# Two transformer blocks on one core: the end of unit 6's routing is moved into the wait for unit 7's projection

## The chip, the cores and the metric

One NeuronCore of a Trainium2 chip runs the whole program. TensorE (PE) multiplies matrices and transposes; VectorE (DVE), ScalarE (ACT) and GpSimd (POOL) work on tiles; SyncE (SP) and GpSimd issue DMAs. The metric is the device time of one execution in microseconds (us). All arithmetic is in 32-bit floats.

## The reference, cut to what matters

The input is 8 rows of 512 tokens with 256 channels. Four layers are added to it in turn, each on a layer norm of what is there:

```
x = x + attention0(norm(x))      # relative positions, 16 heads, softmax over 512 keys
x = x + ffn0(norm(x))            # 256 -> 1024 -> 256, weights changed per row
x = x + attention1(norm(x))      # attends over the 8 rows, at each token position
x = x + moe(norm(x))             # 32 experts, 4 chosen per token, and a shared expert
```

The change lies at the end of attention1 and in the routing of moe. For each token, routing computes 32 scores, keeps two of four groups of experts, takes the best four experts, and scales their outputs by their scores' shares:

```
logits = tokens @ router_weight.T ; scores = sigmoid(logits)
topk_idx = top 4 of (scores + bias), in the two best of four groups
topk_w = scores[topk_idx] / sum * 2.5
mixed = sum over the 4 of expert(token) * topk_w
```

## The kernel before, in words

**Units.** The last two layers are worked in 8 units of 512 tokens (u = 0..7): two rows of the input and half of each row's token positions, as four tiles of 128 tokens. `attend` (L1403) plans the attention of a unit and `routed` (L1427) its routing, which runs beside the attention of the next unit. After unit 7's attention comes its routing with no other unit beside it, then the experts.

**An order written out by hand.** Each step is given a planned time by `at` (L1375). The events are sorted by that time and emitted one after the other; the times only set the order in which each engine's instructions stand. `hop` (L1378) plans a step that is written as a generator: its first part at `first`, the rest at `then`. So TensorE's part can stand early and VectorE's later. In the built program, an instruction that nothing holds can stand earlier on its engine than its event: before the change, the four idle matmuls planned just before unit 7's transposes stand among the last transposes of its attention.

**Attention of unit 7.** `weighted` (L1081) multiplies values by their softmax weights on VectorE, eight times (m = 0..7); the tile `value` has three buffers. `gathered` (L1092) adds their transposes up on TensorE (`ao`), and after the last one ACT copies the sum (`aoT`, L1110). `projected` (L1122), for r = 0 and 1, multiplies by the projection matrix on TensorE (`po`, L1127) and adds the result to x on VectorE.

**Routing.** `measure2` (L1140) takes mean and variance of the four tiles on VectorE (L53, L54, L56) and the root of the variance on GpSimd (`rstd`, L58, a power of -0.5). `norm2` makes `shift` on VectorE and the normed tiles `xn` on ACT (L1149). `turn2` transposes them (`pt`, L1161; `xT`, L1162); `logits` and `scores` follow (L1169, L1173). `route` chooses the experts on VectorE; `count` and `take` place them among all tokens. `send` (L1269) has a first part on TensorE (`pk`, L1276 to L1278) and a second on VectorE: `rule`, `bounds`, `key`, `tops`, `slot` (the rows to which the tokens go), then `eq`, `weight`, and into the tile `pay` the weights and the tokens' numbers (`pay<-weight`, `pay<-dest`). `copied` (L1153) copies `xn` four times into `pay` on ACT, once for each of the four chosen experts. `pay` has one buffer.

**Scatters.** At its end `send` appends 16 scatters to a list. Each is an indirect DMA issued by GpSimd (L941) that writes 128 rows of `pay` to the rows named by `slot`, into a table in DRAM sorted by expert. `pace` (L955) takes two of them off the list and emits them, and makes them wait for the last VectorE instruction emitted so far. In the last unit this extra wait is left out (`free`).

**Fillers.** `busy(n)` (L962) emits n matmuls whose result nobody reads (`idle`, L966). With `behind`, the first waits for the instructions given.

**The seam to the experts.** Unit 6's shared expert is kept for the end (`late_shared`). When unit 7's attention is over, the memory of attention is given back, and SP loads all experts' weights into it (`store`, L1487, eight DMAs). After the routing of unit 7 come the experts' page numbers, unit 6's shared expert, and fillers behind the last scatters (L1503). SP fetches the first sorted rows (`r`, L1514) after all 16 scatters of unit 7 have landed; then 160 steps, one for each page of 128 sorted rows, multiply by their expert's weights.

In line numbers of helpers: all recorded VectorE work of this stage has the line L858.

Of the kernel before, what the change touches and what calls it, by code (L numbers as in the profile page):

```python
# [863 lines left out]
def _l1(nc, tc, a, x, out, ident, mhalf, rows, results, filled, inputs, early):  # L864
# [12 lines left out]
    U = B  # L877
    seen = lambda u: 4 if u % 4 < 2 else 8
    with ExitStack() as ctx:
# [9 lines left out]
        vec = _Recorded(nc.vector)  # L889
# [43 lines left out]
        def after(ins, others):  # L933
            info = mybir.DependencyInfo(mybir.DependencyClass.Sync, mybir.DependencyReason.DATA)
            for o in others:
                tc.add_manual_dep(ins.ins, o.ins.name, info, reason="rows of DRAM")
# [25 lines left out]
        def busy(n, behind=()):  # L962

            idle = quick("idle")
            for _ in range(n):
                ins = nc.tensor.matmul(idle, inputs.wqkv[:, 0, :P], inputs.wqkv[:, 1, :S], start=True, stop=True)  # L966
                if behind:
                    after(ins, behind)
                    behind = ()

        def quick(name):

            return ps_a.tile([P, S], F32, tag="psa", name=name)

        def slow(name):

            return ps_d.tile([P, S], F32, tag="psd", name=name)
# [135 lines left out]
        def two_tiles(u, r):  # L1113
            h, p = divmod(u, 4)
            return x[2 * p + r][:, 2 * h : 2 * h + 2, :]
# [6 lines left out]
        def projected(u, r):  # L1122
            po = slow("po")
            for j in range(2):
                t = 2 * r + j
                for c in range(NK):
                    nc.tensor.matmul(  # L1127
                        po[:, j * H : (j + 1) * H],
                        turned[u][:, c, t * P : (t + 1) * P],
                        inputs.wproj[:, c, :],  # L1130
                        start=c == 0,
                        stop=c == NK - 1,
                    )
            two = two_tiles(u, r).rearrange("p t c -> p (t c)")
            vec.tensor_tensor(two, two, po, ALU.add)


        xn, xT, stats, hids, chosen, scores_of, mores, tabs = {}, {}, {}, {}, {}, {}, {}, {}

        def measure2(u):  # L1140
# [128 lines left out]
        def send(u):  # L1269

            (sel, w, share), tab = chosen.pop(u), tabs.pop(u)
            ps = slow("pk")
            pk = ps[:, : NT * NE].rearrange("p (t e) -> p t e", e=NE)
            by = ps[:, NT * NE : NT * NE + 4 * NE].rearrange("p (i e) -> p i e", e=NE)
            for i in range(4):
                nc.tensor.matmul(by[:, i, :], tab[:, i : i + 1].to_broadcast([NE, P]), ident[:NE, :NE], start=True, stop=True)  # L1276
            nc.tensor.matmul(pk, earlier, sel, start=True, stop=False)
            nc.tensor.matmul(pk, ones, past[:, NT * u : NT * u + NT, :], start=False, stop=True)  # L1278
            yield
            over = lambda i: rule[:, i, :].unsqueeze(1).to_broadcast([P, NT, NE])  # L1280
            rule = sb.tile([P, 4, NE], F32, tag="rule", name="rule", bufs=1)
            vec.tensor_copy(rule, by)
            vec.tensor_copy(bounds[:, u, :], rule[:, 3, :])
            key = sb.tile([P, NT, NE], F32, tag="key", name="key", bufs=1)
            vec.tensor_tensor(key, pk, over(1), ALU.is_lt)
            vec.tensor_tensor(key, key, over(2), ALU.mult)
            vec.tensor_tensor(key, key, pk, ALU.add)
            vec.scalar_tensor_tensor(key, key, 1.0, over(0), ALU.add, ALU.add)
            vec.tensor_tensor(key, key, sel, ALU.mult)
            top = sb.tile([P, NT, 8], F32, tag="tops", name="tops")  # L1290
            for t in range(NT):
                vec.max(top[:, t, :], key[:, t, :])
            slot = sb.tile([P, NT, TOPK], I32, tag="slot", name="slot")
            vec.tensor_scalar(slot, top[:, :, :TOPK], 1.0, None, ALU.subtract)
            eq = sb.tile([P, NT, TOPK, NE], F32, tag="eq", name="eq", bufs=1)
            vec.tensor_tensor(
                eq,
                key.unsqueeze(2).to_broadcast([P, NT, TOPK, NE]),
                top[:, :, :TOPK].unsqueeze(3).to_broadcast([P, NT, TOPK, NE]),
                ALU.is_equal,  # L1300
            )
            vec.tensor_tensor(eq, eq, w.unsqueeze(2).to_broadcast([P, NT, TOPK, NE]), ALU.mult)
            weight = sb.tile([P, NT, TOPK], F32, tag="weight", name="weight", bufs=1)
            vec.tensor_reduce(weight, eq, AX.X, ALU.add)
            vec.scalar_tensor_tensor(
                pay[:, :, :, H + 1], weight, ROUTE_SCALE, share.unsqueeze(2).to_broadcast([P, NT, TOPK]), ALU.mult, ALU.mult
            )
            vec.tensor_copy(pay[:, :, :, H].bitcast(I32), dest[:, NT * u : NT * u + NT, :])
            for t in range(NT):
                for i in range(TOPK):  # L1310
                    waiting.append(
                        partial(scatter, "rows", rows, slot[:, t, i : i + 1].bitcast(U32), pay[:, t, i, :], NS * P - 1)
                    )
# [61 lines left out]
        def at(time, f, *args):  # L1375
            events.append((time, len(events), partial(f, *args)))

        def hop(f, *args, first, then):  # L1378

            made = []  # L1380

            def begin():
                made.append(f(*args))
                next(made[0])

            at(first, begin)
            at(then, lambda: next(made[0], None))

        def prepare(u, t):

            for c in range(NK):
                at(t + 0.6 * c, turn1, u, c)
            for c in range(2 * NK):
                at(t + 1.6 + 1.9 * c + (17 if c >= NK and t > 0 else 0), project, u, c)
            for half in range(2):
                at(t + 9.3 + 1.9 * half + (17 if t > 0 else 0), tokens, u, half)
# [30 lines left out]
        def routed(u, t, n):  # L1427

            at(t + 0.2, measure2, u)
            at(t + 5.0, norm2, u)  # L1430
            if u + 1 == U:
                at(t + 8.19, busy, 4)
            at(t + 8.2, turn2, u)
            at(t + 10.0, logits, u)
            if u + 2 < U or u + 1 == U:
                at(t + 13.4, hidden, u, 0)

            rear = u + 1 == U
            if u + 2 == U:
                late_shared.append(u)  # L1440
            else:
                at(t + (31.0 if rear else 20.0), hidden, u, 1)
            split = route(u)
            at(t + 15.3, next, split)
            at(t + (21.1 if n == 8 else 19.0), next, split, None)
            late = 3.5 if n == 8 else 0.0
            hop(count, u, first=t + 23.4 + late / 2, then=t + 25.0 + late)
            if u + 2 != U:
                at(t + (30.9 if rear else 19.6 if n == 8 else 18.9), gated, u, 0)
            hop(take, u, first=t + 26.0 + late, then=t + 27.8 + late)  # L1450
            if u + 2 != U:
                at(t + (31.5 if rear else 29.5 + late), gated, u, 1)
            for i in range(TOPK):
                at(t + 24.6 + late + 1.1 * i, copied, u, i)
            hop(send, u, first=t + 28.0 + late, then=t + 30.5 + late * 1.8)
            for r in range(2 if u + 2 != U else 0):
                hop(add_shared, u, r, first=t + 32.6 + late + r, then=t + 36.5 + late * 2 + 0.7 * r)
            for i in range(8):
                at(t + 36.0 + late * 1.8 + 2.6 * i, pace, u + 1 == U)


        WAITS = {0: 5, 1: 2, 4: 5, 5: 1, 6: 3, 7: 3}
# [8 lines left out]
        for u in range(U):  # L1471
            t = start[u]
            if u + 2 < U:
                prepare(u + 2, t + 0.01)
            if u + 3 < U:
                normalized(u + 3, t + 7.6)
            attend(u, t)
            routed(u, t + T[u], seen(u + 1) if u + 1 < U else 4)
# [130 lines left out]
        with tc.manual_schedule():  # L1609


            tiles, which, rTs, made, hidTs = {}, {}, {}, {}, {}
# [172 lines left out]
```

## Time and profile before

| what | value |
| --- | --- |
| three runs | 2066.32, 2069.74, 2071.68 us (median 2069.74) |
| the profiled execution | 2061.48 us |
| its span, first to last instruction | 2059.7 us |
| mean granted TensorE clock | 0.978 of full speed |
| busy: PE, DVE, ACT, POOL | 1937.6, 1392.4, 1106.3, 1134.0 us |
| unit 7's attention and routing, until the first fetch of sorted rows | about 1680 to 1778 us |
| first matmul of the experts | 1783.08 us |

A row of the timeline gives the start from the beginning of the span, the duration, the engine, the line, the operation, the tiles (written <- read), and in brackets how long the engine sat idle before it and what released it. A row of the chain of waits gives start, duration, engine, the tile written and the line; the chain is followed back from the end of the window, at each step to what came last. "issue" means that the profile shows nothing that was waited for. In a table of stages the columns are the stage, its length, the busy time (and records) of PE, weight loads, DVE, ACT and POOL, the granted clock, the DMA engines' busy share, and GB/s. Matmuls of 32-bit floats appear as two records each or more, and a few per cent of records can be missing.

### The profile page before, as it was taken

How to read it: one execution, taken by the hardware profiler on the slowest of the kernel's cores; microseconds unless marked ns; L12 is line 12 of the kernel's file. 1: busy time of each engine (PE TensorE's matmuls, PEld its weight loads, DVE VectorE, ACT ScalarE, POOL GpSimd, SP SyncE). 2: the span in 40 equal slices, each digit the busy share in tenths (PEclk: the TensorE clock that was granted, in tenths of full speed). 3: DMA queues.
4: the chain of work that ended last, by engine and by line, in shares of the span. 5: the costliest groups of instructions: out<-in, count | busy, mean ns of one | idle time of the engine just before them, and what ended most of it. 6: DMA issues, size and time to landing. Idle time of an engine off the chain costs nothing. (4 is left out here: it accounts for less than half of the span.)

```text
span 2059.7 us, 49676 instructions
## 1 busy us (share of the span) xinstructions
PE 1937.6 (94%) x18040; PEld 1327.0 (64%) x18040; DVE 1392.4 (68%) x3727; ACT 1106.3 (54%) x2368; POOL 1134.0 (55%) x1334
## 2 busy tenths in 40 slices
PE   7999999999999999999989999999989877899997
PEld 4666666676666766766656666655555444588886
DVE  4677777677777777766776555247876786456666
ACT  3776777767777777776742211344444333144443
POOL 4666777867778677776744111014434443455555
PEclk9999999999999999999999999999999997999999
DMA  9999999999999999999974446801111114557888
GB/s 296 317 317 281 296 300 295 300 285 307 295 298 303 289 310 303 294 298 289 294 224 141 124 127 195 25 0 37 43 38 45 48 45 190 208 164 219 258 262 272
DMA packets 387522, 444.46 MB, mean 216 GB/s; under 512 B 43472, under 2 KB 368080, under 8 KB 386768
## 3 DMA queue, kind: packets, MB, share of 16 engines
q1 hardware_dynamic: 372496, 401.94, 64.3%
q0 software_dynamic: 13824, 38.29, 5.1%
q8 instruction: 146, 2.39, 0.5%
q10 hardware_dynamic: 960, 1.05, 0.2%
q14 instruction: 96, 0.79, 0.1%
HBM read 238.99 MB, written 202.19 MB: 214 GB/s over the span
## 5 line engine op out<-in xcount | busy, mean ns | idle before, releaser
L447 DVE CUSTOM_DVE_ANT_0 e<-sc,winc 128x512 f32<-128x512 f32 x512 | 333.3, 689 | 289.9 <-PE sc L433 174.1
L450 ACT ACTIVATE e<-e,low 128x512 f32<-128x512 f32 x512 | 365.6, 715 | 101.8 <-DVE low L447 100.3
L371 ACT COPY strip<-pa 128x512 f32<-128x512 f32 x512 | 275.2, 591 | 129.1 <-POOL winc L401 53.1
L374 POOL TENSOR_TENSOR own<-aside,strip 128x512 f32<-128x512 f32 x256 | 268.8, 1050 | 113.4 <-ACT strip L371 97.6
L464 DVE COPY et<-et_ps 128x512 f32<-128x512 f32 x512 | 328.5, 683 | 0.7 <-PE et_ps L461 0.7
L421 PE MATMUL sc<-sm,sm 32*128 32x256 f32 (+3 forms) x1792 | 310.0, 436 | 0.7 <-DVE low L447 0.4
L364 PE MATMUL pa<-pos,sm 32*128 32x256 f32 x2048 | 292.1, 401 | 0.1
L941 POOL DMA_INDIRECT rows<-pay,slot x128 | 141.1, 1103 | 220.3 <-issue 207.1
L401 POOL TENSOR_TENSOR winp<-winp,own 128x256 f32<-128x256 f32 x256 | 187.2, 731 | 106.3 <-DMA winp<-shift 83.7
L433 PE MATMUL sc<-ident,winp 128*128 128x128 f32 x1280 | 203.7, 287 | 30.0 <-DMA winp<-shift 29.5
L421 PEld LDWEIGHTS sc<-sm,sm 32*128 32x128 f32 x1792 | 164.3, 185 | 96.8 <-DVE et L464 35.2
L401 POOL TENSOR_TENSOR winc<-winc,own 128x256 f32<-128x256 f32 x256 | 187.1, 731 | 68.3 <-DMA winc<-shift 61.4
L941 POOL DMA_INDIRECT results<-y,r x160 | 156.3, 977 | 119.6 <-ACT y L1560 77.4
L433 PEld LDWEIGHTS sc<-ident,winp 128*128 128x128 f32 x1280 | 137.6, 142 | 108.1 <-issue 57.2
L461 PE MATMUL et_ps<-ident,e 64*128 64x64 f32 x4096 | 184.2, 230 | 1.1 <-DVE et L464 1.1
L364 PEld LDWEIGHTS pa<-pos,sm 32*128 32x128 f32 x2048 | 176.1, 185 | 10.8 <-ACT strip L371 3.9
L58 POOL TENSOR_TENSOR rstd<-var,mhalf 128x2 f32<-128x2 f32 (+1 forms) x56 | 51.0, 911 | 233.8 <-DVE var L56 210.1
L461 PEld LDWEIGHTS et_ps<-ident,e 64*128 64x128 f32 x4096 | 148.8, 140 | 44.1 <-issue 22.1
L473 PE MATMUL ctx_ps<-et,v 128*32 128x128 f32 x4096 | 168.2, 283 | 0.5 <-DVE et L464 0.5
L1540 PE MATMUL pge<-store,rT 128*128 x640 | 166.1, 382 | 1.8 <-DMA r<-rows 0.8
L174 PE MATMUL pq<-xnT,wqk 128*128 128x512 f32 x256 | 132.8, 643 | 0.7 <-PE pv L156 0.7
L738 ACT ACTIVATE hT<-ph,b 128x512 f32<-128x512 f32 x64 | 44.0, 687 | 165.6 <-PE ph L735 165.6
(222 smaller groups left out, 3340.0 us busy)
## 6 DMA issues: line engine op xcount, KB each, us to landing
shift<-strip SPq DMA_DIRECT2D x256, 510.0 KB, 4.3
winp<-shift SPq DMA_DIRECT2D x128, 384.0 KB, 4.9
winc<-shift SPq DMA_DIRECT2D x128, 384.0 KB, 6.3
winp<-shift SPq DMA_DIRECT2D x128, 256.0 KB, 4.3
winc<-shift SPq DMA_DIRECT2D x128, 256.0 KB, 4.4
rows<-empty SPq DMA_DIRECT2D x8, 2640.0 KB, 13.6
r<-rows SPq DMA_DIRECT2D x160, 132.0 KB, 2.7
z<-results SPq DMA_DIRECT2D x32, 512.0 KB, 5.6
```

The source lines that it names most:

```text
L364: nc.tensor.matmul(pa[:, t * W : (t + 1) * W], src[rs, i * P : (i + 1) * P], pos[rs, g, :], start=True, stop=True)
L371: nc.scalar.copy(st[:, 2 * j : 2 * j + 2, :].rearrange("p t w -> p (t w)"), pas[j])
L374: nc.gpsimd.tensor_tensor(own, aside.unsqueeze(2).to_broadcast([P, 2, 2, P]), st[:, :, W - 1 : W].rearrange("p (j t) o -> p t j o", t=2).t ...
L401: nc.gpsimd.tensor_tensor(dst, dst, own[:, t], ALU.add)
L421: nc.tensor.matmul(sc[:, c0:c1], s[side_][rs, cut : cut + P], s[2 + side_][rs, c0:c1], start=c0 == 0, stop=False, skip_group_check=True,)
L433: nc.tensor.matmul(sc[:, m * P : (m + 1) * P], wins[n + 2 * (m - i)][1][:, j, (i - m + 1) * P : (i - m + 2) * P], ident, start=False, stop ...
L447: nc.vector.tensor_tensor_reduce(e, sc, wins[n][0][:, j, :], 1.0, -LOW, ALU.add, ALU.min, low)
L450: nc.scalar.activation(e, e, AF.Exp, bias=low, scale=-1.0, accum_out=totals[b, g // 2][:, i, r : r + 1])
L461: nc.tensor.transpose(bank[:, c : c + 64], e[rs, m * P : (m + 1) * P], ident[rs, rs])
L464: nc.vector.tensor_copy(et[:, f].rearrange("p j m q -> p (j m q)"), bank)
L473: nc.tensor.matmul(ctx_ps[32 * r : 32 * r + 32, i * P : (i + 1) * P], vs[b % 2][:, m, g % 2, g // 2 * 4 + r, :], et[:, :, m, :], start=m = ...
L941: ins = nc.gpsimd.indirect_dma_start(to, bass.IndirectOffsetOnAxis(ap=index, axis=0), source, None, bounds_check=last)
```

## The change

For unit 6 alone, the second part of `send` is cut in two at a new `yield`. Its first piece, `rule` to `slot`, is planned at 46.05 after the start of unit 7, just ahead of unit 7's projections (46.1 and 46.8) and behind its last two `weighted`. Its second piece, `eq` to `pay<-dest`, is planned at 48.3, behind unit 7's `measure2` (48.2). All eight `pace` of unit 6 come after it, from 48.4 on; they stood from 42.3 on, 2.6 apart. In the last unit four fillers become five, and the first waits for the first residual add of unit 7's projection. Other units are unchanged: where `last` is not given, both pieces stand at `then`.

```diff
@@ projected
             vec.tensor_tensor(two, two, po, ALU.add)
+            added[u, r] = vec.last
@@ send
             vec.tensor_scalar(slot, top[:, :, :TOPK], 1.0, None, ALU.subtract)
+            yield
             eq = sb.tile([P, NT, TOPK, NE], F32, tag="eq", name="eq", bufs=1)
@@ hop
-        def hop(f, *args, first, then):
+        def hop(f, *args, first, then, last=None):
...
             at(then, lambda: next(made[0], None))
+            at(then if last is None else last, lambda: next(made[0], None))
@@ routed
             if u + 1 == U:
-                at(t + 8.19, busy, 4)
+                at(t + 8.19, lambda: busy(5, [added[u, 0]]))
             at(t + 8.2, turn2, u)
...
-            hop(send, u, first=t + 28.0 + late, then=t + 30.5 + late * 1.8)
+            if u + 2 == U:
+
+                hop(send, u, first=t + 28.0 + late, then=t + 46.05, last=t + 48.3)
+            else:
+                hop(send, u, first=t + 28.0 + late, then=t + 30.5 + late * 1.8)
...
             for i in range(8):
-                at(t + 36.0 + late * 1.8 + 2.6 * i, pace, u + 1 == U)
+                at(t + (48.4 + 0.01 * i if u + 2 == U else 36.0 + late * 1.8 + 2.6 * i), pace, u + 1 == U)
```

In the built program the order of instructions changes in this place and no other. VectorE: the five last `value` stand in one run, then `rule` to `slot`, the residual adds with their statistics and `var`, then `eq` to `pay<-dest`, then `shift`. GpSimd: `rstd` of unit 7 stands ahead of all 16 scatters of unit 6, where six stood ahead of it. TensorE: four fillers leave the last transposes of `ao`; five stand between `po` and the transposes of `xn`. The orders of ACT and SP are unchanged.

More of the change, by code (lines that the diff above doesn't have):

```diff
@@ L1135, in projected @@
             vec.tensor_tensor(two, two, po, ALU.add)
+            added[u, r] = vec.last
+        added = {}
         xn, xT, stats, hids, chosen, scores_of, mores, tabs = {}, {}, {}, {}, {}, {}, {}, {}
```

## The prediction

> **What bounds the kernel now.** TensorE is busy for 94% of the span on the page, but the change touches only the seam between the last two units and the experts, some 70 us, so I read the chain of waits there (1705 to 1785 us), then the timeline, the clock by stage and the DMA issues. First the chain:
>
> ```profile
> 1718.61 0.27 DVE pay L858 x2
> 1718.88 1.13 DVE value L858
> 1720.05 1.09 PE ao L1098 x8
> 1721.88 0.59 ACT aoT L1110
> 1722.52 2.07 PE po L1127 x8
> 1724.68 0.70 DVE x L858
> ...
> 1729.71 1.05 POOL rstd L58
> 1731.04 0.61 ACT xn L1149
> ...
> 1753.44 0.27 DVE pay L858 x2
> 1753.71 0.59 DVE hid L858
> 1754.35 3.78 PE pu L1321 x4
> ```
>
> VectorE writes unit 6's weights (pay) at 1718.61 and only then the last two values that the projection of unit 7 needs; root, norm, routing and unit 7's pay follow one behind the other. What comes after 1753.44 hangs on that write of pay on two sides: TensorE's last shared experts, and the 16 scatters of unit 7. The timeline of the other engines:
>
> ```profile
> 1720.76 1.24 POOL L941 DMA_INDIRECT rows<-pay,slot  x1 [19.92 <-issue]
> ...
> 1730.79 0.16 DVE L858 SCALAR_TENSOR_TENSOR shift<-mv,rstd 128x4 f32<-128x4 f32 x1 [2.22 <-POOL rstd L58]
> ...
> 1742.52 0.97 POOL L941 DMA_INDIRECT rows<-pay,slot  x1 [0.30 <-issue]
> ...
> 1748.32 1.05 ACT L1154 COPY pay<-xn 128x1024 f32<-128x1024 f32 x1 [0.24 <-DMA rows<-pay,slot]
> ...
> 1754.47 0.97 POOL L941 DMA_INDIRECT rows<-pay,slot  x1 [10.97 <-issue]
> 1757.65 0.98 POOL L941 DMA_INDIRECT rows<-pay,slot  x1 [2.21 <-issue]
> ...
> 1775.54 0.97 POOL L941 DMA_INDIRECT rows<-pay,slot  x1 [0.30 <-issue]
> ```
>
> These are unit 6's first and last scatter, then unit 7's. The fourth copy into pay waits for a DMA: it is let go 5.80 us after unit 6's last scatter was issued (1742.52 to 1748.32). pay has one buffer, so unit 7 may not write it while unit 6's rows are still being read. Now this wait ends 5 us before VectorE comes (1753.44). And the clock (columns: PE, weight loads, DVE, ACT, POOL busy; granted clock; DMA):
>
> ```profile
> 1732.00:1740.00 8.00, 7.73 (x26) 5.62 (x26) 1.25 (x15) 5.13 (x8) 5.87 (x7) 0.50 1.03 416
> 1756.00:1760.00 4.00, 4.00 (x9) 1.92 (x8) 0.69 (x1) 0.00 (x0) 1.95 (x2) 0.56 1.03 405
> 1760.00:1764.00 4.00, 2.51 (x12) 1.87 (x10) 2.11 (x4) 0.00 (x0) 2.92 (x3) 1.00 1.03 407
> ```
>
> After TensorE's 5.40 us pause before the first transpose (1731.70) it runs at 0.50.
>
> **The change, part by part.** The built order shows one place: on VectorE rule..slot move behind the last two values, eq..dest move behind var; on GpSimd the root moves ahead of all 16 scatters of unit 6; on TensorE four idle matmuls leave the last transposes and five come between the projection and the transposes, waiting for the first residual add.
>
> *rule..slot.* They take 1713.83 to 1716.44, 2.61 us. The values' buffers are free in time: they need the transposes of values 3 and 4, done by 1714.4. The last value ends at 1712.69 + 3 x 1.16 = 1716.17 instead of 1721.13; rule..slot then end at 1718.8, and the projection's first half is there at 1724.68 - 4.96 = 1719.7. So they cost nothing: they lie where VectorE waited 3.54 us for po. Without that cover they would cost up to 2.61.
>
> *eq..dest.* They take 1716.44 to 1718.87, 2.43 us. The two together take 2.61 + 2.34 = 4.95 us (by starts) off the way to the projection. var ends at 1728.57 - 4.95 = 1723.6; eq..dest run to 1726.0. GpSimd makes the root in 1.04 to 1.76 us (its rows from 1400 to 1800), with no scatter ahead of it, so by 1725.6. The shift waits for VectorE itself instead of for GpSimd: 1725.9 against 1730.79, gain 4.9. This cover is incomplete: 2.43 takes the place of a wait of 2.22.
>
> *The five idle matmuls.* Three took 2.74 us at full clock, five take some 4.4: from po's end, 1721.4, to 1725.8. The first transpose comes with xn at 1726.15 + 0.6; the pause is 1 us instead of 5.40. Unit 6's rows give the full-clock price: its logits' scores start 2.06 us after the second xT, and I get scores 5.6 us after xn starts, where it is 7.37 here: gain 1.8 at best. Bounds: 0 (clock stays at 0.50), or a loss of 4 if the fillers run at 0.50 (three took 5.49 us so, five 9.2, until 1730.6). I take 1.8, because pauses of 1.67 and 1.74 us before earlier score sums (1630.00, 1682.64) show no slow matmuls behind them. The four idles removed stood where TensorE waited 1.35 us for the value: 0.
>
> The page "TensorE: Matmul & The Clock Gate" of the Trainium skill (Part 1, What's actually happening) says that the clock halves only after an idle window of about 3.4 us. This trace has 0.50 in 1752 to 1756 us after a pause of 3.07 us, so the measurement says that shorter ones can do it too. By the rule the root chain keeps full clock to the end; by the row the 3 us before pc could cost another 1.3 us (the pk group twice as long), which what follows would hide.
>
> *Sum so far:* 4.9 + 1.8 = 6.7 us; unit 7 would be ready to write pay at 1746.7.
>
> *What is late next.* The scatters of unit 6 started at 1720.76, under the projection; now they need dest (1726.0) and stand behind the root on GpSimd. A first scatter starts 0.3 to 0.8 us after what it waits for (1727.16 to 1727.43; 1753.71 to 1754.47): 1726.3 to 1726.8. Fifteen more at the pitch of 1.277 (1757.65 to 1775.54, 14 steps) put the last at 1745.4 to 1746.0 instead of 1742.52. The waits that stretched the old series (for the second residual add and for the root, 2.7 us) are gone, but 5.5 us of start are lost. SP's eight loads of expert weights are released by the projection's end (1726.42 against po's 1726.30), so they start 4.95 us earlier too, and keep the DMA full from about 1724 to 1763: all 16 scatters now land beside them. Landing took 2.4 us without them and 5.5 to 6.3 beside them (DMA issues, by windows); I take the 5.80 of the copy's wait. So pay is free at 1751.2 to 1751.8 and not at 1748.3, and VectorE, which would be there at 1746.7 to 1748, waits 3 to 5 us at weight->pay. Behind that instruction stand dest, both hid products, the shared adds and the experts' numbers on VectorE; TensorE's pu and pos wait for hid; all of ACT's later work waits behind its copies.
>
> *Sum:* pay is written at 1751.3 to 1752.0 instead of 1753.44, mid 1751.7: **-1.7 us**. Behind it both ways shift alike: scatters of unit 7 (first at about 1752.8), and TensorE with pu and pos. TensorE's pause before pu grows from 3.07 to about 8 us, but it ran at 0.50 there already (4.6 us of it, 1754.35 to 1758.98); I take no loss, with 1 us either way as bound, half of a doubled pu. The 2.21 us of idle before unit 7's second scatter has no releaser; should it go, TensorE's side still ends when it did, so nothing is gained; should another one come inside unit 6's series, 1.9 us are lost. On its own execution (2061.48 us, span 2059.70) that makes 2059.8. The three runs shown have a median of 2069.74, 8.3 us above that execution; I put the same difference on the median: **2068.0 us**.
>
> **The rivals.** *The whole gain (6.7 us, 2063.0).* Then unit 6's rows would have to be out by 1746.7. For it: the chain before names no wait on pay. Against: 16 scatters at 1.28 us are 20.4 us and the first needs dest. 7%.
>
> *Slower, by stretched scatters.* Beside VectorE's long products a scatter takes 1.88 to 1.96 us instead of 0.97 (1685.05, 1688.51), 0.9 more each. All 16 now stand beside VectorE's routing of unit 7. From the second stretched one on (2 x 0.9 > 1.7) the gain is gone and the kernel is slower; with four, +2 us (2071.7), with eight, +5.6. Against: ten scatters of unit 6 ran beside such routing (1739 to 1743) at 0.97. 20%. The page "DMA: Bandwidth & Descriptors" (SWDGE vs HWDGE vs iDMA) speaks for this rival: GpSimd writes the descriptors into SBUF, and VectorE locks it out in its 2-port mode. The stretched rows agree in part; the routing's rows show none.
>
> *Nothing, 2069.7.* The fillers or the clock lose what is left, or VectorE comes to the same place at the same time. The built order speaks against it. 8%.
>
> **How the numbers follow.** The forecast has the remaining 65%: -1.7, from -3 (landing 5.5, wake 0.3, clock) to +0.3 (one unexplained stall). About 0.3% (6.2 us) is what a measurement here can tell from no change; only the whole gain passes it, or eight stretched scatters. Faster 7%, slower 7% (a third of the slow rival), the same 86%. For the range: -3 to +2 of the cases is 2066.7 to 2071.7; the three runs spread over 5.36 us, so I add half of that on both sides less what medians take off, 2 us: 2064.5 to 2073.7.
>
> **What would show it.** Right: rstd at 1723.7 and shift near 1725.9; clock 1.00 in 1726 to 1735; unit 6's scatters from 1726.5 to 1745.7 without a gap; the group weight->pay with 3 to 5 us of idle before it, released by the DMA rows<-pay; unit 7's first scatter near 1752.8; the span 2058. Wrong: no wait before pay (the whole gain), issues of 1.9 us among the 16, a clock of 0.50 before the logits, or a projection that isn't 5 us earlier.

## The result, and the profile after

| what | before | after |
| --- | --- | --- |
| median of 20 runs each, taken on the same occasions | 2065.66 us | 2067.23 us |
| ratio after to before | | 1.0012 [0.9996, 1.0028] |
| the profiled execution, and its span | 2061.48, 2059.7 us | 2069.68, 2067.9 us |
| mean granted clock | 0.978 | 0.979 |

The forecast time, 2068.0 us, is 0.8 us from the median. The ratio stands for +2.5 us, with an interval from -0.8 to +5.8, so the forecast step of -1.7 us lies just outside it. That the time itself was hit so closely is luck: the forecast starts from 2069.74 us, the median of three runs, where 20 runs give 2065.66, and the measured step has the other sign. The forecast of no change was right; what made it so has to be looked for.

The chain of waits of the changed kernel in the same place (start, duration, engine, tile, line):

```profile
1713.21 2.07 PE po L1127 x8
1715.37 0.70 DVE x L858
...
1721.34 0.27 DVE pay L858 x2
1721.76 2.08 ACT xn L1151 x4
...
1734.27 3.03 another core or an unknown queue
...
1742.58 13.15 issue
1755.95 0.97 POOL rows L941
```

The order is as planned: unit 6's pay (1721.34) now stands between the residual adds and the normed tiles. Then the chain loses its thread. Three us go to "another core or an unknown queue", though the program has one core, and 13.15 us to "issue". The timeline says what the chain cannot (start, duration, engine, line, operation, in brackets the idle time before and its releaser):

```profile
1719.41 1.35 POOL L58 TENSOR_TENSOR rstd<-var,mhalf 128x4 f32<-128x4 f32 x1 [23.97 <-DVE var L56]
1721.51 0.15 DVE L858 SCALAR_TENSOR_TENSOR shift<-mv,rstd 128x4 f32<-128x4 f32 x1
1722.38 1.05 POOL L941 DMA_INDIRECT rows<-pay,slot  x1 [1.62 <-ACT xn L1151]
...
1737.36 0.07 DVE L858 MEMSET top<- 128x16 f32 x1 [3.09 <-remote]
...
1741.61 0.97 POOL L941 DMA_INDIRECT rows<-pay,slot  x1 [0.30 <-issue]
1742.28 0.29 DVE L858 TENSOR_TENSOR sel<-left,tmp 128x128 f32<-128x128 f32 x1 [3.38 <-remote]
...
1747.20 1.04 ACT L1156 COPY pay<-xn 128x1024 f32<-128x1024 f32 x1 [0.26 <-DMA rows<-pay,slot]
1754.92 0.19 DVE L858 SCALAR_TENSOR_TENSOR pay<-weight,total 128x16 f32<-128x16 f32 x1
1755.95 0.97 POOL L941 DMA_INDIRECT rows<-pay,slot  x1 [13.37 <-issue]
```

The root has no scatter ahead of it, and shift waits for nothing. The 16 scatters of unit 6 run from 1722.38 to 1741.61 without a gap, and pay would be free at 1747.2. But VectorE writes unit 7's pay only at 1754.92, and without a bracket: it did not wait there, it came late. Its routing has holes of 3.09 and 3.38 us, before instructions that need nothing but VectorE's own results. That is new. In the profile of before such holes are absent in this place:

```profile
1742.74 0.07 DVE L858 MEMSET top<- 128x16 f32 x1
...
1743.63 0.29 DVE L858 TENSOR_TENSOR sel<-left,tmp 128x128 f32<-128x128 f32 x1
...
1753.44 0.19 DVE L858 SCALAR_TENSOR_TENSOR pay<-weight,total 128x16 f32<-128x16 f32 x1
```

To compare profiles I count from the start of unit 7's last run of values (1709.77 us in the span of before, 1706.08 of after). "Scores read" is the first instruction of VectorE's choice of experts; "net" is the time from there to pay, without a wait at pay itself.

| kernel | shift | scores read | unit 6's last scatter | unit 7's pay | net | first expert matmul |
| --- | --- | --- | --- | --- | --- | --- |
| before | 21.02 | 28.95 | 32.75 | 43.67 | 14.72 | 73.31 |
| after | 15.43 | 22.82 | 35.53 | 48.84 | 26.02 | 79.68 |

Unit 7 is 5.6 us earlier at shift, 6.1 at the scores, and 5.2 later at pay.

### The profile page after: what moved, and what is told of

The parts are those of the page before. It is cut to its first block, busy times and chain, and to the rows that moved or that the text cites. A ratio compares the mean times of both kernels' runs of the same rounds, so it can differ in the third digit from the quotient of the medians.

```text
span 2067.9 us, 49680 instructions
## 1 busy us (share of the span) xinstructions
PE 1939.2 (94%) x18042; PEld 1328.8 (64%) x18042; DVE 1393.3 (67%) x3727; ACT 1105.2 (53%) x2368; POOL 1133.9 (55%) x1334
```

## Experiments

The kernels ran on three chips: the first four on one (median of before 2078.06 us there), the next four on a second (2058.00), the last four on a third (2079.18). On which chips the first two profiles, of before and after, were taken is not on record.

**The changed kernel again** (no edit).

> The changed kernel once more. Times are counted from the start of the run of the last value products of unit 7's attention (A). In the profile after, VectorE needs 26.0 us from the first step of unit 7's routing (sfc) to weight->pay, where before it needs 14.7; it sits up to 3.4 us waiting for its own results. Theory 1 (pay is the gate, as predicted): this stretch is an accident of one execution; here sfc to weight->pay takes 14.7 us plus a wait of 3 to 5 us released by the scatters, pay is written at about A+41.5, the kernel is 1 to 2 us faster than before. Theory 2 (VectorE's routing is stretched in this order): again more than 22 us from sfc to pay, pay near A+48, and the time is some 3 to 5 us above before. Theory 3 (the stretch comes and goes): the time lies between, with a wide spread.

Measured: ratio 0.9997 [0.998, 1.0015]. Shift at 15.42, scores read at 22.81, pay at 48.25, net 25.44, again without a wait at pay. The lateness of VectorE recurs; it is not an accident of one profile.

**Without the tie.** Four fillers with no wait, as before; the rest of the change stays.

```diff
-                at(t + 8.19, lambda: busy(5, [added[u, 0]]))
+                at(t + 8.19, busy, 4)
```

> The changed kernel with the four fillers as before, tied to nothing; only the weights and slots are moved. If the fillers matter (they hold TensorE's clock until the logits): scores come 1 to 2 us later, counted from xn. If they only postpone the half clock, as the profile after shows (granted 0.50 from 1726 us, logits in 3.67 us as before in 3.2): scores 6.8 to 7.4 us after xn in both, time equal to the changed kernel within 1 us.

Measured: ratio 1.0008 [0.9991, 1.0024]. The fillers stand among the transposes of ao again, and the projection comes 1.7 us later (8.81 against 7.13). From shift to scores it takes 7.61 us against 7.08 with the tie. Scores read at 24.86, pay at 49.44, net 24.58. The tie is not what holds VectorE up.

**The tie alone.** send and pace as before, five fillers tied to the first add (shown against the changed kernel).

```diff
-                hop(send, u, first=t + 28.0 + late, then=t + 46.05, last=t + 48.3)
+            hop(send, u, first=t + 28.0 + late, then=t + 30.5 + late * 1.8)
...
-                at(t + (48.4 + 0.01 * i if u + 2 == U else 36.0 + late * 1.8 + 2.6 * i), pace, u + 1 == U)
+                at(t + 36.0 + late * 1.8 + 2.6 * i, pace, u + 1 == U)
```

> The kernel before with only the five tied fillers, nothing moved on VectorE or GpSimd. Prediction's price: scores 1.8 us earlier, and since pay was free 5 us ahead of VectorE, the time falls by 1.8 us. If the pause after the fillers is still long (the shift comes 10 us after the first residual add, five fillers last 4.4 us), the clock is at 0.50 again and the gain is 0. VectorE's routing takes 14.7 us from sfc to weight->pay if its stretch comes from the changed order (theory 2), and can be stretched here too if it is chance (theory 3).

Measured: ratio 1.0015 [0.9993, 1.0038]. Scores read at 29.86, last scatter at 33.96, pay at 47.98, net 18.12. From shift to scores 7.33 us, where before has 7.62. So tied fillers bring 0.3 us here and 0.5 us in the changed kernel, not 1.8 (three later runs of that order show 0.8 to 1.35; see below). And with the old order of send VectorE is 3 us late as well on this chip, though far less than with the new.

**Expert weights loaded later.** The eight loads are planned behind unit 7's choice of experts, so that the scatters of unit 6 do not run beside them.

```diff
-        for e in range(0, NE, 4):
-            nc.sync.dma_start(store[:, e : e + 4, :], ...)
+        def load_experts():
+            for e in range(0, NE, 4):
+                ins = nc.sync.dma_start(store[:, e : e + 4, :], ...)
+                if e == 0:
+                    after(ins, [vec.last])
+        at(start[U] + 23.35, load_experts)
+        events.sort(key=lambda e: e[:2])
```

> The changed kernel with the eight loads of expert weights held back until unit 7's routing on VectorE is through its second part, so that routing and unit 6's scatters have the DMA to themselves. Theory 1: scatters land 2.4 us after issue instead of 5.6, the copies into pay never wait, pay is written at about A+37.5 (VectorE's routing 14.7 us). Theory 2 with the DMA's load as cause: no waits of VectorE for its own results, the same A+37.5; with the order as cause: stretched as before. The experts then wait for their weights, so the whole time rises by 5 to 15 us and is not read.

Measured (one execution, 2078.16 us): the loads are issued from 34.83 on, 0.7 us before the last scatter. VectorE's holes are there all the same:

```profile
1746.82 0.09 DVE L858 MATCH_VALUE_LOAD left<-top,tmp 128x8 f32 x1 [1.28 <-DVE top L858]
1748.98 0.29 DVE L858 TENSOR_TENSOR sel<-left,tmp 128x128 f32<-128x128 f32 x1 [1.41 <-DVE left L858]
...
1753.92 0.14 DVE L858 TENSOR_SCALAR whole<-whole 32x1 int32<-32x1 int32 x1 [1.68 <-remote]
```

Scores read at 22.35, pay at 46.86, net 24.51. So the holes do not need the big loads. Pay is 1.1 to 2.0 us earlier than in the three other runs of this order with holes (47.96 to 48.84), so a share of the loads in their size is not ruled out.

**Before again, on the second chip** (no edit to the kernel before).

> The kernel before once more, for its trace. In its first profile VectorE's routing of unit 7 had no waits for its own results (14.7 us from sfc to weight->pay). If such waits belong to the changed order only: 14.7 us again, pay at A+43.7. If they come wherever that routing stands beside an unbroken series of scatters: some are seen here too, since ten scatters stand behind the root; 16 to 20 us, and pay at A+45 to 49.

Measured (one execution, 2059.61 us): shift at 20.35, scores read at 28.28, last scatter at 32.08, pay at 44.14, net 15.86. No holes: like the profile of before.

**Unit 6's scatters held back.** All of them behind unit 7's last choice.

```diff
-                at(t + (48.4 + 0.01 * i if u + 2 == U else ...), pace, u + 1 == U)
+                at(t + (67.1 + 0.01 * i if u + 2 == U else ...), pace, u + 1 == U)
```

> The changed kernel with all 16 scatters of unit 6 held back until VectorE has finished the second part of unit 7's routing. The loads of expert weights run as in the changed kernel. If the scatters beside it are what stretches VectorE's routing: no waits for own results, sfc to past 5.2 to 5.5 us instead of 13 to 16, and past at about A+28.3. If it is the expert loads or the place in the program: stretched as before. In either case pay becomes the gate in the open: first scatter at A+29.5, the sixteenth at A+48.7, pay free and written at A+54, released by the DMA rows<-pay; the experts start 5 to 6 us later than in the changed kernel.

Measured (one execution, 2061.49 us): scatters from 30.35 to 49.70, and VectorE at pay:

```profile
1750.76 0.19 DVE L858 SCALAR_TENSOR_TENSOR pay<-weight,total 128x16 f32<-128x16 f32 x1 [15.04 <-DMA rows<-pay,slot]
```

This is the wait that the prediction foresaw, made long by the edit: pay's single buffer is held until unit 6's rows are out. Net 14.69, no holes. Taken alone, the missing holes would show that scatters beside the routing make them; the next two kernels speak against that.

**dest first.** Unit 6's eq to dest directly behind slot, ahead of the residual adds, and two scatters ahead of the root.

```diff
-                hop(send, u, first=t + 28.0 + late, then=t + 46.05, last=t + 48.3)
+                hop(send, u, first=t + 28.0 + late, then=t + 46.05, last=t + 46.06)
...
-                at(t + (48.4 + 0.01 * i if u + 2 == U else ...), pace, u + 1 == U)
+                at(t + ((48.1 if i < 1 else 48.4) + 0.01 * i if u + 2 == U else ...), pace, u + 1 == U)
```

> The changed kernel with eq to dest also ahead of the residual adds, and two of unit 6's scatters ahead of the root on GpSimd. The first residual add then comes 1.5 us later and the shift 0.8 us later (A+16.2), the sixteenth scatter at A+33 instead of A+35.5. Pay as the gate: pay written at A+39 to 40 if VectorE is there by then. Stretch by scatters: it ends 2.5 us sooner than in the changed kernel, past at A+34 to 36, pay at A+46; the time 1 to 2 us below the changed kernel.

Measured: 2050.78 us, ratio 0.9965 [0.9944, 0.9985]. The first scatter comes 3.6 us earlier than in the changed kernel (12.67 against 16.30), the last at 32.89; the residual add pays 1.34 us for it (10.63 against 9.29). Pay at 39.32, of it 0.90 us wait for unit 6's rows, and the first expert matmul at 70.09, 3.2 to 3.8 us earlier than in the two profiles of before without holes. There are no holes here either, though 14 scatters run unbroken behind the root, eight of them beside the routing. The 3.2 to 3.8 us are about half of the 7.2 us between the medians; the interval goes from 3.1 to 11.5 us, so the profile does not contradict the time, nor does it account for all of it.

**Eight fillers** in place of five, in the changed kernel.

```diff
-                at(t + 8.19, lambda: busy(5, [added[u, 0]]))
+                at(t + 8.19, lambda: busy(8, [added[u, 0]]))
```

> The changed kernel with eight fillers instead of five behind the first residual add. Five ended 1.1 us before the first transpose and the clock fell to 0.50 some 4 us later, so the logits took as long as before. If the pause of 1.1 us and the thin transposes cost the clock: with eight (until 0.1 us after the first xn is there) the clock stays at 1.00 and scores come 5.6 us after xn starts instead of 6.8. If the thin transposes alone do it, the clock falls as before and scores come 6.8 to 7.4 us after xn. The time is not read.

Measured (one execution, 2057.86 us). The stage 1726 to 1732 us lies at the same place in both kernels (they differ by 0.06 us there). Columns: stage, length, busy PE, weight loads, DVE, ACT, POOL; granted clock; DMA share; GB/s. First with five fillers (after):

```profile
1718.00:1721.00 3.00, 3.00 (x8) 1.14 (x6) 2.83 (x8) 0.00 (x0) 1.35 (x1) 1.00 0.88 247
1721.00:1724.00 3.00, 1.38 (x5) 0.53 (x5) 0.63 (x4) 2.07 (x4) 1.32 (x2) 1.00 1.02 413
...
1726.00:1732.00 6.00, 6.00 (x17) 3.93 (x18) 2.48 (x22) 2.18 (x3) 4.50 (x5) 0.50 1.03 411
```

and with eight:

```profile
1721.00:1724.00 3.00, 3.00 (x10) 1.33 (x9) 0.69 (x4) 2.07 (x4) 1.26 (x2) 1.00 1.03 419
...
1726.00:1732.00 6.00, 4.78 (x20) 2.52 (x19) 3.98 (x34) 2.92 (x4) 4.48 (x6) 1.00 1.02 405
```

Five leave TensorE busy for 1.38 of the 3 us in which xn is made, and the clock falls to 0.50 behind it. Eight close the hole, and the clock stays at 1.00. With eight the transposes also run in one stretch, so this run does not part the pause from the thin transposes behind it. From shift to scores it takes 5.73 us instead of 7.08. And this is the changed order, with eight fillers, in a profile without holes:

```profile
1747.79 0.19 DVE L858 SCALAR_TENSOR_TENSOR pay<-weight,total 128x16 f32<-128x16 f32 x1 [4.09 <-DMA rows<-pay,slot]
```

Pay at 41.65 after 4.09 us of wait; net 16.08. The last scatter was issued at 35.63, 6.0 us before.

What stayed open then: after and the first four kernels had the holes, the next four did not, whatever their order, and neither had before. Order and chip were mixed. So four kernels were put on one chip.

**The changed kernel, on the third chip.**

> The changed kernel once more, beside the kernel before and two others on one chip, because the runs that showed VectorE's routing stretched and those that did not came from two occasions. Measured from the start of unit 7's last run of values; the stretch is read as the time from VectorE's read of the scores to its write of the weights into pay, 14.7 to 15.9 us in the kernel before and 24.5 to 26.0 us in the changed one. If the stretch belongs to the new order (all 16 scatters in one unbroken series beside the routing): 24 to 26 us again, pay written 48 to 49 us after that start, no wait on pay. If it belongs to the chip or the occasion, as it would if the run before it of the kernel with eight fillers (20.2 us, the last 4 of them the wait for pay) is typical: about 18.5 us, pay written at 41 to 42 us, just behind the landing of unit 6's last scatter, with 2 to 4 us of idle before it released by the DMA; the time then 2 us below the kernel before.

Measured: ratio 1.0012 [0.9993, 1.0031]; net 25.96, pay at 47.96, no wait on it.

**Before, on the third chip.**

> The kernel before, unchanged, for a profile beside the others. If the stretch belongs to the order: 14.7 to 15.9 us from scores to pay, pay written at 43.7 to 44.2 us. If to the chip: as long or as short as in the others of this occasion; 18 us or more would show that the old order is stretched too.

Measured (one execution, 2082.0 us): net 18.59, pay at 46.90, first expert matmul at 76.97. The old order has holes here too:

```profile
1757.07 0.29 DVE L858 TENSOR_TENSOR tmp<-sfc,rank 128x128 f32<-128x128 f32 x1 [0.90 <-DVE tmp L858]
...
1758.57 0.07 DVE L858 MEMSET top<- 128x16 f32 x1 [0.71 <-DVE top L858]
```

They are small, and the last ends 2.6 us after the issue of its last scatter (1755.95). So neither pure theory holds: the chip or the occasion decides whether there are holes, the order how many.

**dest first, on the third chip.**

> The version with eq to dest ahead of the residual adds and two scatters ahead of the root, once more: it was 0.35% faster than the kernel before. If that was the order's doing: pay written at 39 to 40 us, scores to pay 15.9 us, ratio 0.996 to 0.998 to the kernel before, 4.4 to 4.8 us off at pay. If VectorE was only undisturbed by chance or by the chip: scores to pay 24 us on an occasion where the changed kernel shows so, pay at 48 us and no gain.

Measured: ratio 0.9997 [0.9978, 1.0015]; pay at 46.73, net 23.26. The gain seen on the second chip is gone. It is the same program, and up to the scores the two profiles agree within 0.01 us (23.46 and 23.47 from the start). VectorE from there, first on the second chip:

```profile
1730.11 0.47 DVE L858 MAX8 top<-tmp 128x8 f32<-128x32 f32 x4
1730.65 0.07 DVE L858 MEMSET top<- 128x16 f32 x1
...
1731.54 0.29 DVE L858 TENSOR_TENSOR sel<-left,tmp 128x128 f32<-128x128 f32 x1
1731.87 0.87 DVE L858 TENSOR_TENSOR past<-past,sel 128x32 f32<-128x32 f32 x4
...
1742.46 0.19 DVE L858 SCALAR_TENSOR_TENSOR pay<-weight,total 128x16 f32<-128x16 f32 x1 [0.90 <-DMA rows<-pay,slot]
```

then on the third:

```profile
1749.80 0.47 DVE L858 MAX8 top<-tmp 128x8 f32<-128x32 f32 x4 [0.92 <-DVE tmp L858]
1751.27 0.07 DVE L858 MEMSET top<- 128x16 f32 x1 [1.00 <-DVE top L858]
...
1755.47 0.29 DVE L858 TENSOR_TENSOR sel<-left,tmp 128x128 f32<-128x128 f32 x1 [2.68 <-remote]
1756.18 0.19 DVE L858 TENSOR_TENSOR past<-past,sel 128x32 f32<-128x32 f32 x1 [0.42 <-DVE sel L858]
...
1767.59 0.19 DVE L858 SCALAR_TENSOR_TENSOR pay<-weight,total 128x16 f32<-128x16 f32 x1
```

The instructions last as long in both. Only the time between an instruction and its successor that reads its result has grown.

**dest first with eight fillers, on the third chip** (the edits of dest first and of eight fillers together).

> The same with eight fillers in place of five. Eight held the clock and brought the scores 1.4 us earlier than five. If the landing of unit 6's last scatter is what holds pay here, nothing more comes of it: pay at 39 to 40 us as with five, the wait before it 2 to 2.5 us in place of 0.9, the same time as with five. If VectorE is what holds it: pay 0.9 to 1.4 us earlier, at 38 us, and the time lower by that.

Measured: ratio 0.9995 [0.9975, 1.0016]; scores read at 22.18, 1.3 us earlier than with five, pay at 46.71, the same within 0.02 us.

```profile
1760.57 0.29 DVE L858 TENSOR_TENSOR sel<-left,tmp 128x128 f32<-128x128 f32 x1 [4.73 <-remote]
```

This sel starts 34.61 us from the start, exactly when it did with five fillers: the hole before it grew by what was gained. Neither expected case (a longer wait for the rows, or pay earlier by what the fillers bring) came. It looks as if something that ends at a fixed time behind the scatters lets VectorE go; what that is, no run shows.

### The profiles together

"Overlap" is the time from the scores' reading to the issue of unit 6's last scatter; "late" is the net time less 15.3, the mean of the five profiles without holes (14.72, 15.86, 14.69, 14.96, 16.08).

| profile with holes | overlap | net | late | late / overlap | pay |
| --- | --- | --- | --- | --- | --- |
| before, third chip | 3.8 | 18.59 | 3.3 | 0.87 | 46.90 |
| tie alone | 4.1 | 18.12 | 2.8 | 0.68 | 47.98 |
| dest first, third chip | 9.5 | 23.26 | 8.0 | 0.84 | 46.73 |
| dest first with eight | 10.7 | 24.53 | 9.2 | 0.86 | 46.71 |
| without tie | 12.2 | 24.58 | 9.3 | 0.76 | 49.44 |
| after | 12.7 | 26.02 | 10.7 | 0.84 | 48.84 |
| changed kernel again | 12.7 | 25.44 | 10.1 | 0.80 | 48.25 |
| weights loaded later | 13.2 | 24.51 | 9.2 | 0.70 | 46.86 |
| changed kernel, third chip | 13.6 | 25.96 | 10.7 | 0.79 | 47.96 |

In all nine, routing that runs beside the scatters of the unit before is 0.7 to 0.9 us late for each us of overlap (up to 1.35 us of it is pk on a TensorE that the pause has slowed: rule waits 2.61 us for it in all nine, and 1.26 to 2.61 in the five). In the five without holes the same overlap costs nothing: 9.4 us of it in dest first on the second chip, 14.2 with eight fillers. The DMA view separates the same two sets. Its row for the scatters gives no time to landing in any of the nine, here after:

```profile
rows<-pay,slot POOLq DMA_INDIRECT x128
```

and 2.4 or 2.5 us in the five, here dest first on the second chip:

```profile
rows<-pay,slot POOLq DMA_INDIRECT x128, 2.5
```

The traces tell more. They hold the updates of semaphores, by which an engine or a landing DMA lets a waiting engine go. Up to the first scatter of the program all 14 have 13,616 updates by DMAs, 16 for each of the 851 DMAs issued till then. Of the 8,096 that the 506 DMAs after it should make, the nine lack 3,765 to 4,130 and the five 14 to 37. VectorE's own updates are missing too: the nine hold 2,369 to 2,390 of some 2,700, the five all. And the holes lie at these updates. Taking as a hole each wait of more than 0.15 us for VectorE's own semaphore alone, the nine have 71 between the scores and pay. In 66 the update is recorded 0.02 to 0.06 us before the waiting instruction starts, long after the instruction before it has ended; in the other five its record is missing. In the routing of the five profiles without holes it stands within 0.02 us of that end. So VectorE does not start late: its semaphore's update comes late.

What differs between the two sets is open: the chip, the occasion, or the recording, which loses updates in one set and not in the other, from the first scatter on. That the recording itself holds the updates up is a rival that nothing here settles; every run on record has its span and clock from such a recording, the timed ones too. No run here takes the scatters away on a chip with holes, so that they cause the holes is argued from the table, not shown. The timed runs have the same sign as the profiles: dest first gains 0.35% on the second chip and nothing on the third.

## Why the prediction was right, and where it was wrong

*The projection and the shift, 4.95 and 4.9 us earlier.* Right. Against the profile of before, shift is 5.6 us earlier; against before on the second chip 4.9 (20.35 to 15.43). The residual add is 5.0 earlier there (14.25 to 9.29). rule to slot cost nothing, and the root came without a scatter ahead of it.

*Five fillers, 4.4 us long, a pause of 1 us, 1.8 us gained.* The length (4.46) and the pause (1.13) were right; the gain was 0.5 (7.62 to 7.08), the same in its repetition, and 0.8 to 1.35 in three other runs with this order up to the scores (scatters held back 6.79, weights loaded later 6.62, third chip 6.27). The step that failed is "pauses of 1.67 and 1.74 us before earlier score sums show no slow matmuls behind them". Those pauses were followed by score sums of 2.18 us in one stretch, this one by four transposes of 0.33 us with 0.16 between them, and the clock fell to 0.50 at 19.35 us from the start. Where it fell later, at 20.24, the gain was the 1.35. Eight fillers, which take away both the pause and the thin transposes, brought 1.9 us (7.62 to 5.73), which is what I had counted on for five; which of the two cost the clock is not shown.

The page "TensorE: Matmul & The Clock Gate" of the Trainium skill (Part 1, What's actually happening) lets the clock fall after an idle window of some 3.4 us that runs freely. The granted clock here does change at multiples of 3.41 us (1701.53, 1725.43, 1732.25 in after). But TensorE was busy for 2.22 of the 3.41 us ahead of the fall at 1725.43, so here the measurement decides: it fell without an idle window. My other row against the page, the pause of 3.07 us, was misread: the clock had fallen at 1749.25, and that pause ran from 1751.28 to 1754.35.

*The 16 scatters from 1726.3 to 1726.8, the last at 1745.4 to 1746.0, landing 5.8 us.* In the frame of before that is 16.5 to 17.0 and 35.6 to 36.2 from the start. Measured 16.30 and 35.53, with the fourth copy let go 5.59 us later. Right.

*VectorE at 1746.7 to 1748 at pay, waiting 3 to 5 us; pay at 41.5 to 42.2 from the start, 1.7 us earlier.* Without holes this is what happens. With eight fillers the wait was 4.09 us and pay stood at 41.65: 2.0 and 2.5 us earlier than in the two profiles of before without holes. With five fillers (scores read at 22.82, net 15.3) VectorE would come at 38.1 and wait 3.5 us; the unmodified change has no profile without holes, so that is worked out and not measured. In its own profile the step fails: VectorE came 10.7 us late, there was no wait, and pay was 1.1 to 1.9 us later than in before on the third chip (47.96 to 48.84 against 46.90). The sign that I had set for being wrong, no wait before pay, came, but not for the whole gain: VectorE was late.

*Behind pay both ways shift alike, no loss.* This term was too small. With eight fillers pay is 2.0 and 2.5 us earlier, but the first expert matmul only 0.5 and 1.1 (72.78 against 73.31 and 73.88). TensorE's clock was at 0.50 from 1759.46 to 1762.88 there, and the pg behind the experts' numbers took 3.57 us (at 1759.25), in before 1.80 (at 1765.30). In all 1.4 to 1.5 us are lost, against the bound of 1 us.

*The rival of stretched scatters.* It named the right meeting, scatters beside VectorE's routing, and looked for the price on the wrong engine. The scatters kept 0.97 us and their pitch of 1.28. VectorE paid. My evidence against it, ten scatters beside such routing at 0.97, was read from GpSimd's rows of a profile without holes; only 3.8 us of routing, and four of the ten, lay beside each other there.

So the time stayed the same for two reasons, one for each set of profiles. Without holes the scatters' landing takes back all but 2 us of the 6, and the slow TensorE behind pay more than half of these 2. With holes VectorE takes back all of it and 1 to 2 us more. The change lets the series of scatters end 3.4 us later (32.13 to 35.53), and VectorE is let go near that end. That the later end is the cause is argued, and "weights loaded later" speaks against it: its series ends at 35.52, and its pay stands at 46.86. In neither set does the projection set unit 7's pay.

The version with dest first ends the series at 32.9 and keeps the early projection. It was faster than before on one chip and the same on the other. The changed kernel was not timed on the chip where dest first was faster, so which of the two is better there is not shown.

(The lower end of the range, worked out again from its own terms, is 2064.7 us and not 2064.5; nothing hangs on it.)

## What to carry to other kernels

Before work is made early, look for what its first write must wait for: here a single buffer, free only when the last scatter out of it has landed, kept all but 2 of 6 us. Move only what the early step needs; whatever starts a long series of DMAs has to keep its place. When a series of DMAs comes to lie beside another engine's chain of small instructions, read the waits of both engines, and read them on more than one chip. Before two profiles are compared, count whether both hold the same records.

## What the runs showed of the hardware

VectorE stood still for up to 4.73 us between an instruction and its successor that reads the result. This was seen in nine of fourteen profiles, beside GpSimd's scatters or up to 3.4 us after the last of them was issued; the durations of the instructions did not change, nor did those of the scatters. The loads of expert weights can be taken away from most of the series without ending it. The page "Perfetto Trace Analysis" of the Trainium skill (Per-engine timelines) says that a semaphore update spreads after the end that the profiler reports for an instruction. The traces agree that the time lies there: the late update is recorded 0.02 to 0.06 us before the successor starts. The same nine profiles lack about half of the landings' updates from the first scatter on, so it is not ruled out that the recording has a part in this.

The same program was 0.35% faster than before on one chip and the same on another, with profiles that agree to 0.01 us until the scores. An interval from one chip speaks for that chip.
